# A two-layer recurrent kernel: the selective scan's product with C on GpSimd while expert tiles run

## The chip, the cores and the metric

The program runs on one core of one Trainium2 chip. The metric is the device time of one execution in microseconds. Three runs of the kernel before gave 2524.88 us in the middle, from 2520.57 to 2531.61.

## What is computed

Two layers follow one another on x of shape (4, 1024, 256), all in fp32. Layer 0 is an attention with a Fourier feature map and a gate. Layer 1 is a selective scan (512 channels, 16 states) times the SiLU of a mixture of 8 experts, two experts per token, one after the other. The change lies in layer 1:

```python
def step(h, inp):
    dt_t, B_t, C_t, u_t = inp
    dA = jnp.exp(dt_t[:, :, None] * A)
    h = h * dA + (dt_t * u_t)[:, :, None] * B_t[:, None, :]
    y = jnp.einsum('bcs,bs->bc', h, C_t)
    return (h, y)
...
for i in range(TOP_K):
    eo = _selected_expert(boost, topk_idx[:, :, i], W1, b1, W2, b2)
    outs.append(eo)
    if i < TOP_K - 1:
        boost = boost + ALPHA * eo
...
g = _silu(experts(xn))
x = x + s * g
```

## The kernel before

Time is cut into 8 blocks of 512 tokens (`NBLK`, `TB`), channels into 4 chunks of 128 (`NDI`), two chunks to a half (`UNIT`). One scan step is one (block, half, state): 8 x 2 x 16 = 256 steps.

For a step, `decay` (L588) loads B and C of that state, broadcast over the partitions, into `bcs` (SyncE's queue, 3 buffers) and lets ScalarE make `da` = exp(dt A) (4 buffers). `scan_step` (L606) then gives VectorE four instructions: `h` = dt u times B (L623, 128x1024), two scans (L626, 128x512 each, in place in `h`), and `da` = h times C (L634, 128x1024). `h` has one buffer. Where a block begins a sequence, a small copy keeps the tail of `h` (L631). TensorE adds `da` into `y` by eight accumulating transposes (L637). `y` has one buffer of two PSUM banks; at the end of a unit of 16 steps `end_unit` (L660) multiplies it with the gate on VectorE (L662), and only then the next unit's first matmuls (L617) may write it.

The experts work on slots: `scatter` (L849) writes tokens to rows sorted by expert, with GpSimd's indirect DMA; `all_tiles` (L922) runs 23 slot tiles of 256 rows. For a tile, `fetch` (L870) loads the expert's weights `we` (indirect, GpSimd, 3 buffers) and the rows `xs` (GpSimd's queue, 2 buffers), `hidden_layer` transposes `xs` (`pxs`), copies it (`xst`) and makes `ph` and `ht`; `output_layer` makes `po` on TensorE, adds the bias on VectorE (`es`, L919) and stores it through GpSimd's queue (L920). Then `gather` (L860, buffers `ga`: 8) fetches rows back per token, VectorE makes the second expert's input `x1` (L958, 4 buffers) and updates `xn_all` (L959), `scatter` writes `x1`, and a second round of 23 tiles follows. The last gathers feed L970, a normalization and the output.

`cycle` (L1059) interleaves these: after layer 0 is closed (`l0.close()`), each cycle emits decays up to six steps ahead, two scan steps, up to two pieces of the next unit's preparation (`beside`, L690), and one piece of the experts (`quota=(0, 0, 2, 1)`, L1123), so one slot tile beside two scan steps. That is the order of the program. The framework that builds it orders each engine's queue when the program is built, and among what it takes to be ready it follows the program's order. So `es` of a tile can stand between the two scans of a step, or eight transposes to `y` can be split around `ph`. On the chip each queue runs strictly in that order: an instruction that waits holds all those behind it, DMA issues on SyncE's and GpSimd's queues too.

PSUM's eight banks: `ps_y` 2, `ps_acc` 2 (layer 0's attention alone), `ps_bank` 4.

Of the kernel before, what the change touches and what calls it, by code (L numbers as in the profile page):

```python
# [13 lines left out]
F32 = mybir.dt.float32  # L14
U32 = mybir.dt.uint32
AF = mybir.ActivationFunctionType
ALU = mybir.AluOpType
AX = mybir.AxisListType
PSUM = bass.MemoryType.PSUM
DRAM = bass.MemoryType.DRAM  # L20

P = 128
NB, L, D = 4, 1024, 256
TB = 512
# [10 lines left out]
TS = 256  # L35
# [24 lines left out]
def kernel(  # L60
# [3 lines left out]
    nc = tc.nc  # L64
# [22 lines left out]
    def tokens(ap):  # L87
        return ap.rearrange("(t p) d -> p t d", p=P)
# [7 lines left out]
    def accumulate(ps, pairs):  # L96
        for i, (lhs, rhs) in enumerate(pairs):
            nc.tensor.matmul(ps, lhs, rhs, start=i == 0, stop=i == len(pairs) - 1)  # L98
# [4 lines left out]
    scan = ctx.enter_context(tc.tile_pool(name="scan1", bufs=2))  # L103
    small = ctx.enter_context(tc.tile_pool(name="small", bufs=2))
    ps_y = ctx.enter_context(tc.tile_pool(name="ps_y", bufs=1, space=PSUM))
    ps_acc = ctx.enter_context(tc.tile_pool(name="ps_acc", bufs=2, space=PSUM))
    ps_bank = ctx.enter_context(tc.tile_pool(name="ps_bank", bufs=4, space=PSUM))

    def bank(name):
        return ps_bank.tile([P, TB], F32, name=name, tag="bank")  # L110


    l0 = ExitStack()
    wp = l0.enter_context(tc.tile_pool(name="w0", bufs=1))
    keep = l0.enter_context(tc.tile_pool(name="keep0", bufs=1))
    work = l0.enter_context(tc.tile_pool(name="work0", bufs=7))

    def fetch_x(j):
# [11 lines left out]
        out=bias_s, in_=rows_a.rearrange("a d -> (a d)").partition_broadcast(P)  # L130
# [384 lines left out]
    UNIT = NDI // 2  # L515
# [85 lines left out]
            )  # L601
        decays[j, hf, n] = (bcs, da)

    sums = {}

    def scan_step(j, hf, n):  # L606

        first = j % (L // TB) == 0
        dtu = units[j, hf][1]
        bcs, da = decays.pop((j, hf, n))  # L610
        if n == 0:
            u = blocks[j][1]
            sums[j, hf] = ps_y.tile([P, NT, UNIT * P], F32, name=f"y_{j}{hf}", tag="y")
            for t in range(NT):
                for w in range(UNIT):
                    c = UNIT * hf + w
                    nc.tensor.matmul(  # L617
                        sums[j, hf][:, t, w * P : (w + 1) * P], u[:, c, t * P : (t + 1) * P],
                        skip[:, c, :], start=(t % 2, w) == (0, 0), stop=False,
                    )  # L620
        y = sums[j, hf]
        h = scan.tile([P, UNIT, TB], F32, name=f"h_{j}{hf}_{n}", tag="h", bufs=1)
        nc.vector.tensor_tensor(h, dtu, bcs[:, 0:1, :].to_broadcast([P, UNIT, TB]), ALU.mult)  # L623
        for w in range(UNIT):
            c = UNIT * hf + w
            nc.vector.tensor_tensor_scan(  # L626
                h[:, w, :], da[:, w, :], h[:, w, :],
                0.0 if first else h_tail[:, c, n : n + 1], ALU.mult, ALU.add,
            )
        if first:  # L630
            nc.vector.tensor_copy(  # L631
                h_tail[:, UNIT * hf : UNIT * (hf + 1), n : n + 1], h[:, :, TB - 1 : TB]
            )
        nc.vector.tensor_tensor(da, h, bcs[:, 1:2, :].to_broadcast([P, UNIT, TB]), ALU.mult)  # L634
        for t in range(NT):
            for w in range(UNIT):
                nc.tensor.matmul(  # L637
                    y[:, t, w * P : (w + 1) * P], da[:, w, t * P : (t + 1) * P], ident,
                    is_transpose=True, start=False, stop=(n, t % 2, w) == (NS - 1, 1, UNIT - 1),
                )  # L640
# [49 lines left out]
    def beside(j, hf):  # L690
# [11 lines left out]
        elif j + 1 < NBLK:  # L702
# [8 lines left out]
    slots_in = [dram.tile([NST * TS, D], F32, name=f"slots_in{k}", tag=f"slots_in{k}") for k in range(2)]  # L711
    slots_out = [dram.tile([NST * TS, D], F32, name=f"slots_out{k}", tag=f"slots_out{k}") for k in range(2)]
# [4 lines left out]
            out=slots_in[k].rearrange("(a p) d -> p a d", p=P),  # L717
            in_=blank.unsqueeze(1).to_broadcast([P, NST * TS // P, D]),
# [4 lines left out]
    def needs(later, earlier):  # L723
        tc.add_manual_dep(
            later.ins, earlier.ins.name,
            mybir.DependencyInfo(mybir.DependencyClass.Sync, mybir.DependencyReason.DATA),
        )

    def experts(rp, moe):
# [11 lines left out]
        for e in range(NE):  # L741
# [4 lines left out]
            out=before_m, in_=ones, compare_op=ALU.is_ge, fill=0.0, base=-1,  # L746
# [102 lines left out]
        def scatter(k, t, src):  # L849

            i = nc.gpsimd.indirect_dma_start(
                out=slots_in[k], out_offset=IndirectOffsetOnAxis(ap=slot[:, k, t : t + 1], axis=0),
                in_=src, in_offset=None,
            )
            for o in scattered[k]:
                tc.declare_no_dep(i.ins, o.ins, reason="rows of different tokens")
            needs(i, blanked[k])
            scattered[k].append(i)

        def gather(k, t):  # L860
            g = moe.tile([P, D], F32, name=f"ga_{k}_{t}", tag="ga", bufs=8)
            nc.gpsimd.indirect_dma_start(
                out=g, out_offset=None, in_=slots_out[k],
                in_offset=IndirectOffsetOnAxis(ap=slot[:, k, t : t + 1], axis=0),
            )
            return g
# [3 lines left out]
        def fetch(k, i):  # L870

            w = moe.tile([P, WCAT], F32, name=f"we_{k}_{i}", tag="we", bufs=3)
            nc.gpsimd.indirect_dma_start(
                out=w, out_offset=None, in_=wcat,
                in_offset=IndirectOffsetOnAxis(ap=wrow[:, k, i : i + 1], axis=0),
            )
            xs = moe.tile([P, 2, D], F32, name=f"xs_{k}_{i}", tag="xs")
            got = nc.gpsimd.dma_start(out=xs, in_=tokens(slots_in[k][i * TS : (i + 1) * TS, :]))
            for o in scattered[k]:
                needs(got, o)  # L880
            fetched[k, i] = (w, xs)
# [27 lines left out]
        def output_layer(k, i):  # L909
            w, ht = fetched.pop((k, i))[0], hidden.pop((k, i))  # L910
            we2 = w[:, W1C : W1C + W2C].rearrange("p (f n) -> p f n", n=D)
            b2 = w[:, W1C + W2C + B1C :]
            ps = bank(f"po_{k}_{i}").rearrange("p (u d) -> p u d", u=2)
            for u in range(2):
                accumulate(
                    ps[:, u, :], [(ht[:, f, u * P : (u + 1) * P], we2[:, f, :]) for f in range(NHC)]
                )
            es = moe.tile([P, 2, D], F32, name=f"es_{k}_{i}", tag="es")
            nc.vector.tensor_tensor(es, ps, b2.unsqueeze(1).to_broadcast([P, 2, D]), ALU.add)  # L919
            nc.gpsimd.dma_start(out=tokens(slots_out[k][i * TS : (i + 1) * TS, :]), in_=es)  # L920

        def all_tiles(k):  # L922
            for i in range(2):
                fetch(k, i)
            yield "N"
            for i in range(NST + 1):
                if i:
                    output_layer(k, i - 1)
                if i < NST:
                    hidden_layer(k, i)  # L930
                if i + 2 < NST:
                    fetch(k, i + 2)
                yield "N"

        for t in range(NTT):
            scatter(0, t, xn_all[:, t, :])
            if t % 8 == 7:
                yield "N"
        yield from all_tiles(0)

        def tile_gathers(k):

            got = {}
            for j in range(NBLK + 1):
                if j < NBLK:
                    got[j] = [gather(k, t) for t in range(j * NT, (j + 1) * NT)]
                    yield None
                if j:
                    yield j - 1, got.pop(j - 1)

        for found in tile_gathers(0):
            if found is None:
                yield "N"
                continue
            j, gs = found
            for t, g in zip(range(j * NT, (j + 1) * NT), gs):
                x1 = moe.tile([P, D], F32, name=f"x1_{t}", tag="x1", bufs=4)
                nc.vector.scalar_tensor_tensor(x1, g, 0.5, xn_all[:, t, :], ALU.mult, ALU.add)  # L958
                nc.vector.scalar_tensor_tensor(  # L959
                    xn_all[:, t, :], g, val[:, 0, t : t + 1], xn_all[:, t, :], ALU.mult, ALU.add  # L960
                )
                scatter(1, t, x1)
        yield from all_tiles(1)
        for found in tile_gathers(1):
            if found is None:
                yield "N"
                continue
            j, gs = found
# [150 lines left out]
    rp = ctx.enter_context(tc.tile_pool(name="routes1", bufs=1))  # L1119
    moe = ctx.enter_context(tc.tile_pool(name="moe1", bufs=2))  # L1120
    moe_s.add(experts(rp, moe))
    while not scans.done():
        cycle(quota=(0, 0, 2, 1))  # L1123
    turn_half(NBLK - 1, 1)
# [75 lines left out]
```

## Time and profile before

| what | value |
|---|---|
| median of three runs | 2524.88 us |
| the profiled execution's own time | 2525.45 us |
| its span | 2523.5 us |
| first round of tiles, about | 1600 to 1930 us |
| gathers and second scatters | 1930 to 2060 us |
| second round of tiles | 2060 to 2375 us |
| last gathers, normalization, output | 2375 to 2523.5 us |
| scan steps (L634) in the two rounds of tiles | 49 and 51 |
| loading of `bcs`, issue to landing, in the first round | 5.5 us (median) |
| loading of `we` there | 7.8 us (median) |

The span is what the engines' records cover; the time is what a run reports, 1.95 us more. Starts are counted from the span's start. Busy time of an engine in a stretch against the stretch's length tells how near it is to being the bound there; a chain of waits tells which work ended last at each point.

### The profile page before, as it was taken

To read this page: it belongs to the slowest core of one execution; us is meant where nothing else is said; L and a number is where in the kernel's file an instruction comes from. 1 tells how busy PE (TensorE), PEld (TensorE's weight loads), DVE (VectorE), ACT (ScalarE), POOL (GpSimd) and SP (SyncE) were. 2 spreads that over 40 slices of the span, in tenths; PEclk is the share of its full clock that TensorE was granted. 3 is DMA by queue.
4 is the path that set the end of the run, shared out by engine and by line. 5 is a ranking of instruction groups with operands and counts; after the bars stand their busy time and mean duration, and the time that the engine had idled before them with its cause. 6 is when DMAs were issued, how large, how long until landed. Compare 5 with 4: busy or idle time off the path is not lost.

```text
span 2523.5 us, 25853 instructions
## 1 busy us (share of the span) xinstructions
PE 1894.3 (75%) x9052; PEld 1256.5 (50%) x9052; DVE 2037.3 (81%) x2878; ACT 1334.4 (53%) x2098; POOL 474.0 (19%) x499
## 2 busy tenths in 40 slices
PE   7789795798878888779896865588996458898630
PEld 3335453345554445544455543476784347677520
DVE  4542549999798787887899999699898889989786
ACT  5763457877866767767664343334553333445310
POOL 1001100101000110100001013321224752122241
PEclk8779797699888899979898876799998579999755
DMA  8001123323223223323234463666676447667624
GB/s 287 17 5 46 47 64 84 92 75 78 78 79 106 71 63 82 95 59 96 78 97 131 100 180 99 193 213 219 198 231 196 122 140 224 195 223 227 183 65 158
DMA packets 135777, 315.24 MB, mean 125 GB/s; under 512 B 12240, under 2 KB 39248, under 8 KB 129760
## 3 DMA queue, kind: packets, MB, share of 16 engines
q1 hardware_dynamic: 101456, 168.52, 25.2%
q0 software_dynamic: 34192, 145.08, 16.5%
q8 instruction: 71, 1.16, 0.2%
q14 instruction: 58, 0.48, 0.1%
HBM read 259.56 MB, written 54.00 MB: 124 GB/s over the span
## 4 chain that ended last, share of the span: by engine, by line
DVE 41%; PE 36%; ACT 8%; issue 7%; DMA 5%; POOL 3%; SPq 0%; POOLq 0%; DVEq 0%; ACTq 0%
DVE h L626 14%; DVE h L623 6%; DVE da L634 5%; PE ph L98 4%; PE pa L502 3%; PE ph_b L98 3%; PE po L98 3%; PE y L637 3%; PE py_b L98 2%; PE kv L471 2%; DVE fs_q L442 2%; DVE fs_k L442 2%; DVE u L541 2%; PE pi L98 1%; PE pz L98 1%
## 5 line engine op out<-in xcount | busy, mean ns | idle before, releaser
L637 PE MATMUL y<-ident,da 128*128 128x128 f32 x2048 | 319.0, 303 | 236.0 <-DVE da L634 224.5
L190 ACT ACTIVATE da<-dt,neg_a 128x512 f32<-128x512 f32 x512 | 336.5, 717 | 237.8 <-PE y L637 134.9
L637 PEld LDWEIGHTS y<-ident,da 128*128 128x128 f32 x2048 | 262.2, 156 | 333.3 <-issue 150.6
L626 DVE TENSOR_TENSOR_SCAN h<-da,h_tail,h 128x512 f32<-128x512 f32 x256 | 318.0, 1273 | 32.6 <-ACT da L190 27.8
L626 DVE TENSOR_TENSOR_SCAN h<-da,h 128x512 f32<-128x512 f32 x256 | 302.3, 1213 | 25.5 <-ACT da L190 20.2
L623 DVE TENSOR_TENSOR h<-dtu,bcs 128x1024 f32<-128x1024 f32 x256 | 313.0, 1222 | 5.1
L634 DVE TENSOR_TENSOR da<-h,bcs 128x1024 f32<-128x1024 f32 x256 | 312.5, 1221 | 5.0
L98 PE MATMUL ph<-xst,we 128*128 128x256 f32 x736 | 173.7, 390 | 12.4 <-ACT xst L894 10.9
L98 PE MATMUL po<-we,ht 128*128 128x256 f32 x736 | 172.5, 387 | 3.4 <-DVE es L919 3.1
L182 ACT ACT_TABLE_LOAD x130 | 166.8, 1283 | 2.9 <-PEq L1185 0.8
L98 PEld LDWEIGHTS ph<-xst,we 128*128 128x128 f32 x736 | 138.1, 193 | 39.3 <-ACT xst L894 22.0
L98 PE MATMUL ph_b<-x3t_b,w_b 128*128 128x512 f32 x256 | 134.0, 667 | 25.7 <-DMA w_b<-in_w_dram 15.9
L98 PEld LDWEIGHTS po<-we,ht 128*128 128x128 f32 x736 | 138.7, 195 | 29.2 <-issue 4.3
L906 ACT ACTIVATE ht<-ph,we 128x256 f32<-128x256 f32 x184 | 79.7, 469 | 118.6 <-PE ph L98 117.7
L502 PE MATMUL pa<-fs_q,kvp 128*32 128x512 f32 x512 | 130.3, 736 | 12.9 <-ACT fs_q L190 12.7
L98 PE MATMUL py_b<-w_b,ht_b 128*128 128x256 f32 x512 | 118.9, 392 | 3.7 <-DVE fs_k L442 2.0
L442 DVE SCALAR_TENSOR_TENSOR fs_q<-fs_q,fq 128x512 f32<-128x512 f32 x128 | 81.5, 683 | 46.4 <-ACT fs_q L441 46.0
L442 DVE SCALAR_TENSOR_TENSOR fs_k<-fs_k,fk 128x512 f32<-128x512 f32 x128 | 81.0, 681 | 41.4 <-ACT fs_k L441 41.3
L98 PEld LDWEIGHTS py_b<-w_b,ht_b 128*128 128x128 f32 x512 | 100.1, 197 | 26.9 <-issue 7.2
L441 ACT ACTIVATE fs_q<-fq,round_c 128x512 f32<-128x512 f32 x128 | 79.8, 688 | 62.6 <-PE fq L433 32.2
L471 PE MATMUL kv<-fs_k,v_a 128*32 128x256 f32 x1024 | 88.8, 475 | 27.6 <-ACT fs_k L190 27.6
L433 PE MATMUL fq<-qt_a,bd 32*128 32x512 f32 x256 | 99.5, 717 | 11.8 <-DVE fs_q L442 6.9
(223 smaller groups left out, 3327.6 us busy)
## 6 DMA issues: line engine op xcount, KB each, us to landing
bcs<-bcd SPq DMA_DIRECT2D x256, 512.0 KB, 5.2
x<-in_x_dram POOLq DMA_DIRECT2D x23, 512.0 KB, 6.2
slots_in<-blank SPq DMA_DIRECT2D x2, 5888.0 KB, 31.3
xs<-slots_in POOLq DMA_DIRECT2D x46, 256.0 KB, 4.6
slots_out<-es POOLq DMA_DIRECT2D x46, 256.0 KB, 4.0
w_b<-in_w_dram POOLq DMA_DIRECT2D x16, 512.0 KB, 5.2
w_b<-in_w_dram POOLq DMA_DIRECT2D x32, 256.0 KB, 3.1
x_mid<-x POOLq DMA_DIRECT2D x8, 512.0 KB, 3.4
```

What stands on the lines that cost most here:

```text
L98: nc.tensor.matmul(ps, lhs, rhs, start=i == 0, stop=i == len(pairs) - 1)
L182: nc.scalar.preload_act_table_set({"E": "natural_log_exp_and_others", "S": "silu_and_others"}[which])
L190: in_turn(nc.scalar.activation(out, in_, func, **kw))
L433: nc.tensor.matmul(ps[r], bd_s[rows, par, :], qt[rows, m, :], start=True, stop=True)
L441: nc.scalar.activation(fs[r][:, 0, :], ps[r], AF.Identity, bias=round_c)
L442: nc.vector.scalar_tensor_tensor(fs[r][:, 1, :], fs[r][:, 0, :], -ROUND, ps[r], ALU.add, ALU.subtract)
L471: nc.tensor.matmul(kv[b][r // 2][32 * g : 32 * g + 32, r % 2, :, :], v[:, t, h * DH : (h + 2) * DH], f[:, :, m, par, :], start=(s, t, r % ...
L502: nc.tensor.matmul(pa[b, s][32 * r : 32 * r + 32, :], kvp[b][:, e, 4 * m + r, par, :], fs[r][:, e, :], start=(par, e) == (0, 0), stop=(par ...
L623: nc.vector.tensor_tensor(h, dtu, bcs[:, 0:1, :].to_broadcast([P, UNIT, TB]), ALU.mult)
L626: nc.vector.tensor_tensor_scan(h[:, w, :], da[:, w, :], h[:, w, :], 0.0 if first else h_tail[:, c, n : n + 1], ALU.mult, ALU.add,)
L634: nc.vector.tensor_tensor(da, h, bcs[:, 1:2, :].to_broadcast([P, UNIT, TB]), ALU.mult)
L637: nc.tensor.matmul(y[:, t, w * P : (w + 1) * P], da[:, w, t * P : (t + 1) * P], ident, is_transpose=True, start=False, stop=(n, t % 2, w) ...
```

## The change

Once layer 0 is closed, its two PSUM banks (`ps_acc`, now opened with layer 0's pools) become a buffer `hb`, and a second buffer for `h` is opened for odd states; the room for it comes from `ga` (8 to 6 buffers) and `x1` (4 to 2). From then on dt u B is written to `hb`, and the scans read it there and write `h`. While `all_tiles` runs, from the second of its pieces to the last (`beside_tiles`), the product with C is two GpSimd instructions of 128x512, each after its own scan, in place of one VectorE instruction of 128x1024. Loads of `xs` and stores of `es` go to SyncE's queue.

```diff
-    ps_acc = ctx.enter_context(tc.tile_pool(name="ps_acc", bufs=2, space=PSUM))
...
     l0 = ExitStack()
+    ps_acc = l0.enter_context(tc.tile_pool(name="ps_acc", bufs=2, space=PSUM))
...
-    sums = {}
+    sums, alone, beside_tiles = {}, [], [False]
...
-        h = scan.tile([P, UNIT, TB], F32, name=f"h_{j}{hf}_{n}", tag="h", bufs=1)
-        nc.vector.tensor_tensor(h, dtu, bcs[:, 0:1, :].to_broadcast([P, UNIT, TB]), ALU.mult)
+        if alone and n % 2:
+            h = alone[1].tile([P, UNIT, TB], F32, name=f"h_{j}{hf}_{n}", tag="h")
+        else:
+            h = scan.tile([P, UNIT, TB], F32, name=f"h_{j}{hf}_{n}", tag="h", bufs=1)
+
+        hb = h
+        if alone:
+            hb = alone[0].tile([P, UNIT, TB], F32, name=f"hb_{j}{hf}_{n}", tag="hb")
+        nc.vector.tensor_tensor(hb, dtu, bcs[:, 0:1, :].to_broadcast([P, UNIT, TB]), ALU.mult)
         for w in range(UNIT):
             c = UNIT * hf + w
             nc.vector.tensor_tensor_scan(
-                h[:, w, :], da[:, w, :], h[:, w, :],
+                h[:, w, :], da[:, w, :], hb[:, w, :],
                 0.0 if first else h_tail[:, c, n : n + 1], ALU.mult, ALU.add,
             )
+            if alone and beside_tiles[0]:
+                nc.gpsimd.tensor_tensor(da[:, w, :], h[:, w, :], bcs[:, 1, :], ALU.mult)
...
-        nc.vector.tensor_tensor(da, h, bcs[:, 1:2, :].to_broadcast([P, UNIT, TB]), ALU.mult)
+        if not (alone and beside_tiles[0]):
+            nc.vector.tensor_tensor(da, h, bcs[:, 1:2, :].to_broadcast([P, UNIT, TB]), ALU.mult)
...
-            g = moe.tile([P, D], F32, name=f"ga_{k}_{t}", tag="ga", bufs=8)
+            g = moe.tile([P, D], F32, name=f"ga_{k}_{t}", tag="ga", bufs=6)
...
-            got = nc.gpsimd.dma_start(out=xs, in_=tokens(slots_in[k][i * TS : (i + 1) * TS, :]))
+            got = nc.sync.dma_start(out=xs, in_=tokens(slots_in[k][i * TS : (i + 1) * TS, :]))
...
-            nc.gpsimd.dma_start(out=tokens(slots_out[k][i * TS : (i + 1) * TS, :]), in_=es)
+            nc.sync.dma_start(out=tokens(slots_out[k][i * TS : (i + 1) * TS, :]), in_=es)
...
             yield "N"
+            beside_tiles[0] = True
             for i in range(NST + 1):
...
+            beside_tiles[0] = False
...
-                x1 = moe.tile([P, D], F32, name=f"x1_{t}", tag="x1", bufs=4)
+                x1 = moe.tile([P, D], F32, name=f"x1_{t}", tag="x1", bufs=2)
...
     moe_s.add(experts(rp, moe))
+    alone += [
+        ctx.enter_context(tc.tile_pool(name="hb1", bufs=1, space=PSUM)),
+        ctx.enter_context(tc.tile_pool(name="h1", bufs=1)),
+    ]
```

## The prediction

> **What bounds the kernel now.** I read the page's busy shares first, then busy time by stretch, then both engines' order of time inside the tiles, then waits and transfers. Over the whole span:
>
> ```profile
> PE 1894.3 (75%) x9052; PEld 1256.5 (50%) x9052; DVE 2037.3 (81%) x2878; ACT 1334.4 (53%) x2098; POOL 474.0 (19%) x499
> L623 DVE TENSOR_TENSOR h<-dtu,bcs 128x1024 f32<-128x1024 f32 x256 | 313.0, 1222 | 5.1
> L634 DVE TENSOR_TENSOR da<-h,bcs 128x1024 f32<-128x1024 f32 x256 | 312.5, 1221 | 5.0
> ```
>
> VectorE is the busiest, GpSimd idles 81%, and the product that moves costs 1221 ns a step. But the change acts in the two rounds of tiles alone. Busy time by stretch (length, TensorE, its weight loads, VectorE, ScalarE, GpSimd, granted clock, DMA share, GB/s):
>
> ```profile
> 1600.00:1930.00 330.00, 280.71 (x1448) 234.10 (x1448) 282.50 (x283) 152.68 (x267) 75.71 (x77) 0.93 0.67 209
> 2060.00:2375.00 315.00, 275.58 (x1420) 231.71 (x1420) 289.50 (x289) 150.25 (x263) 63.22 (x66) 0.93 0.66 208
> ```
>
> TensorE (85% and 87%) stands right behind VectorE (86% and 92%): two near-bounds, not one. VectorE in order of time, then TensorE where it is dense:
>
> ```profile
> 1670.71 2.34 DVE L626 TENSOR_TENSOR_SCAN h<-da,h 128x512 f32<-128x512 f32 x2
> 1673.08 0.17 DVE L631 COPY h_tail<-h 128x2 f32<-128x2 f32 x1
> 1673.16 1.22 DVE L634 TENSOR_TENSOR da<-h,bcs 128x1024 f32<-128x1024 f32 x1
> 1674.41 1.22 DVE L623 TENSOR_TENSOR h<-dtu,bcs 128x1024 f32<-128x1024 f32 x1
> 1675.74 2.34 DVE L626 TENSOR_TENSOR_SCAN h<-da,h 128x512 f32<-128x512 f32 x2
> 1678.12 0.17 DVE L631 COPY h_tail<-h 128x2 f32<-128x2 f32 x1
> 1678.19 1.22 DVE L634 TENSOR_TENSOR da<-h,bcs 128x1024 f32<-128x1024 f32 x1
> 1679.45 1.22 DVE L623 TENSOR_TENSOR h<-dtu,bcs 128x1024 f32<-128x1024 f32 x1
> 1680.59 0.68 DVE L919 TENSOR_TENSOR es<-po,we 128x512 f32<-128x512 f32 x1
> 1681.19 2.33 DVE L626 TENSOR_TENSOR_SCAN h<-da,h 128x512 f32<-128x512 f32 x2
> ```
>
> ```profile
> 1864.69 3.62 PE L98 MATMUL po<-we,ht 128*128 128x256 f32 x16
> ...
> 1874.07 3.65 PE L98 MATMUL po<-we,ht 128*128 128x256 f32 x16
> ...
> 1883.53 3.65 PE L98 MATMUL po<-we,ht 128*128 128x256 f32 x16
> ```
>
> A cycle is two steps and a tile. On VectorE it takes 1681.19 - 1670.71 = 10.5 us without a gap. On TensorE, packed, 9.4 us (9.38 and 9.46 between starts of `po`). So where VectorE sets the pace at most 1.1 us a cycle can go before TensorE does. Last, who holds SyncE's queue in the later half (1480 to 2450 us), and the loads of `bcs` in the first round:
>
> ```profile
> SPq L593 <- DVE da L634: 740.6, 121, 19.6
> ```
>
> ```profile
> bcs<-bcd SPq DMA_DIRECT2D x46, 512.0 KB, 5.5
> ```
>
> SyncE spends most of its time with a `bcs` load at its head that waits for the product three steps back; whatever is queued behind it waits too. The whole page puts a long idle time of GpSimd's queue down to `xs` waiting for transposes of the tile before:
>
> ```profile
> POOL xs L878 <- PE pxs L890: 281.1, 36, 21.4
> ```
>
> This wait now goes to SyncE.
>
> **What the Trainium skill says.** "SBUF — State Buffer", Who interferes with whom: a VectorE instruction with two SBUF inputs contends with a GpSimd instruction that reads SBUF, and the later one blocks until the first is done; one with at most one SBUF input doesn't. So the scans, which read `hb` in PSUM, are free of it, and L623 (`dtu` and `bcs`) is not. "PSUM — Partial Sum Buffer", Specifications: VectorE reads and writes PSUM, GpSimd neither; so `h` stays in SBUF. "DMA: Bandwidth & Descriptors", Issuing engines are not separate DMA queues: all queues share the same 16 engines; moving a DMA only saves issue time. The trace of before shows neither contention nor a GpSimd product; the shared engines it shows (67% busy in the tiles, from both queues).
>
> **The change part by part.**
>
> *The product leaves VectorE.* 49 + 51 steps x 1.22 us = 122 us of VectorE's time go in the tiles. What it is worth is set by TensorE. I cut 1640:1920 and 2060:2380 into thirty slices of 20 us; in twelve (1640, 1660, 1680, 1700, 1820, 1880, 2080, 2100, 2120, 2140, 2220, 2320) VectorE is busy 19.3 us or more and TensorE at most 18.5. These 240 us are VectorE's; TensorE is busy 187 us of them. At 9.4 in place of 10.5 us a cycle they become 240 x 9.4 / 10.5 = 215: 25 us gained. Ceiling: TensorE's whole idle time there, 53 us; floor: 0. I take 25. In the other eighteen slices TensorE is the bound or both wait for a chain (the loads of `xt` of 8 us), and I count nothing.
>
> *GpSimd's halves.* No row of before has such an operation (the 128x4 ones of L202 are powers). Price from "GPSIMD Engine Reference", 3.1: 4497 ns for 2048 fp32 elements of an add, so an estimate of 1.12 us for 512; with a fixed part left over, up to 1.35. A cycle has four: 4.5 to 5.4 us, and a `we` issue of 1.5 us (L873), less the two issues of 0.73 us that leave: GpSimd is at most 7 us busy in 9.4. Half 0 runs beside the second scan (1.23 us). Half 1 becomes ready when VectorE goes on to the next L623: they collide on the read port. If L623 goes first, half 1 runs beside the next scan, and VectorE loses 0.1 to 0.3 us a step (3.8 + 0.2 = 4.0 us, plus half of `es`, 4.3, still under TensorE's 4.7). If half 1 goes first each time, L623 waits 1.2 us: 5.05 us as before, and nothing is gained. I take the first, because L623 follows the scan on its own engine without a semaphore.
>
> *dt u B to PSUM, scans from PSUM.* `es`, which reads PSUM, takes 0.68 us for 512 elements against 1.22 us for 1024 in SBUF, so 0.07 us an access, about 0.2 us a step; hidden under TensorE in the tiles, at most 4 us in all outside them (some 22 steps in the gathers and at the end).
>
> *`da`, `y` and `bcs` come later.* The product is ready 1.4 us (free port) to 2.7 us (after L623) after the second scan, against 1.25. Behind it stand TensorE's `y`, ScalarE's next `da` (4 buffers: scans 2.5 + product 2.6 + `y` 1 to 5 + `da` 1.3 to 3 = 7 to 13 us, in four steps of 4.7, covered), and the next load of `bcs` on SyncE. That loop is issue 0.36 + load 5.5 + L623 1.26 + scans 2.46 + product 2.6 + semaphores 0.2 = 12.4 us for 3 buffers: 4.1 us a step (3.7 before), under 4.7 but with only 0.6 left. At a unit's end `y`, L662 and L617 come up to 1.4 us later, six times: 8 us, half of it covered by a tile's matmuls. I take 4 us lost.
>
> *`xs` and `es` to SyncE.* Issue time is nothing (0.36 us each). In SyncE's queue each stands between loads of `bcs`. `xs` of tile i+2 is released by `pxs` of tile i and needed two cycles later: 18.8 - 4.6 = 14 us slack. `es` (two buffers) likewise. They don't suffer; `bcs` behind them can, see the rivals. On GpSimd they no longer stand ahead of `we`, of `branch` and of the halves. At the first round's start `xs` waited there 3.80 us for the last scatter, and a store of `branch` behind it (1601.94) held ScalarE and so VectorE for 13.44 us. Without `xs` it issues about 3 us sooner: 3 us gained.
>
> *Fewer `ga` and `x1`.* From 1929 to 2055 GpSimd issues 64 indirect DMAs almost back to back, about 4 us a token tile, and sets the pace. With two `x1`, the tile after next needs this one's scatter landed: 3.0 us (median) + L958 0.43 + a scan in the way 1.5 = 5 us for two tiles, under the 8 us that GpSimd needs; but VectorE stands at L958 where the scatter is late (8.8 us in three waits already with four). Bounds 0 to 15 us; I take 4 lost.
>
> Sum: -25 - 3 + 4 + 4 = -20 us. Against the profiled execution's 2525.45 (span 2523.5 and 1.95 around it) this gives 2505; the median of the runs, 2524.88, lies 0.6 below, within rounding.
>
> **Rivals.**
>
> A, the full yield: VectorE, relieved, also prepares units sooner and clears L662 for L617 at once, so TensorE's idle time in the twelve slices goes wholly (53 us): about 2477. For it: L617 waited 14.8 us for L662 in 1600:1930. Against: loads of `xt` and the collision of L623 stay.
>
> B, the port takes it back: half 1 wins each time, a step stays 5.05 us, VectorE sets the pace as before. What is left is 3 us gained and 4 + 4 lost: 2530. For it: nothing in the trace excludes it. Against: the order above.
>
> C, the other side: SyncE's queue becomes the bound. The `bcs` loop has 12.4 us of work for three steps. When a wait of `xs` or `es` stands ahead of `bcs`, or 256 KB of either ahead of it on the same ring, the loop grows. From 4.7 us a step, that is an average delay of 1.2 us a cycle, it sets the pace; from 5.25 (2.3 us a cycle) the tiles are slower than before. At 3 us a cycle it is 11.3 us: +0.8 us in some 23 VectorE cycles and +1.9 in some 10 packed TensorE cycles, 37 us; with 4 + 4 - 3 it is 2567, at 2.5 us about 2550. I take 2555. For it: SyncE's head waits above and the mean wait of 7.8 us (281.1 / 36) for `pxs`, inherited. Against: the queues follow the same built order, so most such waits are over before `bcs` is due.
>
> **How the numbers follow.** The likeliest (0.42): 2505, own range 2490 to 2517. A 0.13, B 0.21, C 0.24. A measurement tells 0.5% from no change, 12.6 us. Faster: 0.36 of the likeliest, A, 0.02 of B = 0.51. Same: 0.06, 0.15 of B, 0.01 of C = 0.22. Slower: 0.04 of B, 0.23 of C = 0.27. The range leaves out the best part of A and the worst third of C, some 0.15 in all: 2473 to 2557.
>
> **What would show it.** L634 on VectorE down from 256 to some 156, about 200 GpSimd products of 1.1 to 1.4 us; L623 not longer than 1.3 us (B: up to 2.5). Starts of `po` in packed stretches still 9.4 us apart, and more such stretches; TensorE 90% or more in both rounds. Rounds of tiles some 12 us shorter each; gathers not over 135 us. Wrong if VectorE waits for `bcs` at L623 by more than 1 us a step (C), if L623 lengthens (B), or if L958 waits more than 15 us in the gathers.

## The result, and the profile after

The changed kernel takes 2537.93 us (median of 12 runs, 2529.20 to 2542.60), the kernel before in the same call 2524.52 us. The ratio is 1.0040, 95% interval 1.0026 to 1.0055: by this some 10 us slower (the ratio comes from all runs of both, not from the two medians, which differ by 13.4), where 20 us faster was forecast. The profiled span grew from 2523.5 to 2536.3 us.

Engine shares and groups of instructions of after (x count, busy us, mean ns, idle before):

```profile
PE 1894.2 (75%) x9052; PEld 1254.4 (49%) x9052; DVE 1967.2 (78%) x2782; ACT 1334.4 (53%) x2098; POOL 691.6 (27%) x599
L638 POOL TENSOR_TENSOR da<-h,bcs 128x512 f32<-128x512 f32 x192 | 309.3, 1631 | 183.6 <-DVE h L633 152.5
L630 DVE TENSOR_TENSOR hb<-dtu,bcs 128x1024 f32<-128x1024 f32 x140 | 189.7, 1355 | 34.4 <-DMA bcs<-bcd 33.2
L644 DVE TENSOR_TENSOR da<-h,bcs 128x1024 f32<-128x1024 f32 x160 | 194.9, 1218 | 2.3
L640 DVE COPY h_tail<-h 128x2 f32<-128x2 f32 x128 | 39.1, 305 | 2.8
```

The move happened: 96 of 256 products left VectorE and came back as 192 halves on GpSimd. VectorE's busy time fell by 70 us. Busy time by stretch, the columns as before:

```profile
1600.00:1930.00 330.00, 273.75 (x1395) 227.32 (x1396) 255.94 (x243) 145.54 (x258) 192.51 (x128) 0.92 0.71 214
2060.00:2375.00 315.00, 264.50 (x1349) 221.81 (x1350) 250.07 (x246) 138.60 (x245) 187.68 (x123) 0.91 0.66 202
```

VectorE went from 86% and 92% to 78% and 79%. TensorE did not go up into the room that was made: 83% and 84% here, and where the tiles are under way the same as before (262.6 of the 300 us from 1640, against 263.1 of those from 1630). No engine is a full bound now. The trace gives the time by stage, by the starts of the first and last `es` of each round (us):

| stage | before | after | difference |
|---|---|---|---|
| start to the first `es` of round 1 | 1633.0 | 1645.0 | +12.0 |
| round 1 | 290.4 | 287.8 | -2.6 |
| last `es` of round 1 to first of round 2 (gathers, second scatters, first tile) | 157.7 | 159.5 | +1.8 |
| round 2 | 291.6 | 294.3 | +2.7 |
| last `es` of round 2 to the end | 150.8 | 149.7 | -1.1 |

Each column is one execution. In the kernel before with two `x1` buffers (below), which leaves the program of the rounds as it is, they take 293.6 and 294.0 us, 5.6 us more than in before. A few microseconds in a round therefore mean little by themselves.

So two questions: why the rounds gained nothing from 70 us less of VectorE, and where the 12.7 us outside them come from.

**A step in the rounds.** VectorE of after in order of time, same stretch as before, then GpSimd beside it:

```profile
1672.44 0.67 DVE L929 TENSOR_TENSOR es<-po,we 128x512 f32<-128x512 f32 x1
1673.02 0.99 DVE L640 COPY h_tail<-h 128x2 f32<-128x2 f32 x1
1673.92 1.22 DVE L630 TENSOR_TENSOR hb<-dtu,bcs 128x1024 f32<-128x1024 f32 x1
1675.28 2.33 DVE L633 TENSOR_TENSOR_SCAN h<-da,hb 128x512 f32<-128x512 f32 x2
1677.64 0.23 DVE L640 COPY h_tail<-h 128x2 f32<-128x2 f32 x1
1677.79 1.22 DVE L630 TENSOR_TENSOR hb<-dtu,bcs 128x1024 f32<-128x1024 f32 x1
1679.14 2.33 DVE L633 TENSOR_TENSOR_SCAN h<-da,hb 128x512 f32<-128x512 f32 x2
```

```profile
1671.49 2.50 POOL L638 TENSOR_TENSOR da<-h,bcs 128x512 f32<-128x512 f32 x2 [2.59 <-DVE h L633]
1674.13 1.85 POOL L883 DMA_INDIRECT we<-in_wcat_dram,wrow  x1
1676.58 3.55 POOL L638 TENSOR_TENSOR da<-h,bcs 128x512 f32<-128x512 f32 x2 [0.59 <-DVE h L633]
1680.44 3.55 POOL L638 TENSOR_TENSOR da<-h,bcs 128x512 f32<-128x512 f32 x2 [0.31 <-DVE h L633]
```

A step without `es` now takes 3.86 us (1679.14 - 1675.28), against 5.03 before: for such a step the forecast's 4.0 was close. The pair of halves is 2.50 us where nothing stands against it and 3.55 where L630 started first: the second half then waits for L630's end. Where the second half started first (1673.02), what waits on VectorE is the copy of 128x2: it ends when GpSimd does, 0.99 us in place of 0.17. L630 itself came behind GpSimd in 17 of the 91 steps of the rounds, and then took 1.5 to 3.2 us.

**What TensorE waits for.** The dense step is faster, and the round is not. The waits of TensorE by name in the two rounds (us in total, times, longest; round 1, then round 2), of before and of after:

```profile
PE y L617 <- DVE ys L662: 14.8, 2, 10.3
PE y L637 <- DVE da L634: 12.7, 7, 4.0
...
PE y L617 <- DVE ys L662: 20.6, 3, 10.3
PE y L637 <- DVE da L634: 5.7, 3, 2.3
```

```profile
PE y L617 <- DVE ys L672: 19.8, 3, 6.8
PE y L647 <- POOL da L638: 5.0, 3, 2.1
...
PE y L617 <- DVE ys L672: 22.8, 3, 9.4
PE y L647 <- POOL da L638: 5.0, 3, 2.1
```

Before, TensorE waited 18.4 us for the product and 35.4 us for `ys` at the ends of units; after, 10.0 and 42.6. Sums: 53.8 and 52.6 us. The wait for the product fell by 8.4 us and that at the unit ends grew by 7.2. The kernel with two `x1` buffers, whose rounds have the program of before, differs from before by about as much the other way (25.1 for the product and 28.4 us for `ys`), so these two differences explain nothing alone. All of TensorE's waits come to 67 us before and 69 after.

One unit end of after, all three engines in order of time:

```profile
1689.39 3.56 POOL L638 TENSOR_TENSOR da<-h,bcs 128x512 f32<-128x512 f32 x2 [0.60 <-DVE h L633]
1690.91 0.38 PE L647 MATMUL y<-ident,da 128*128 128x128 f32 x2
1691.95 2.33 DVE L633 TENSOR_TENSOR_SCAN h<-da,hb 128x512 f32<-128x512 f32 x2
1694.20 0.67 DVE L929 TENSOR_TENSOR es<-po,we 128x512 f32<-128x512 f32 x1
1694.79 0.97 DVE L640 COPY h_tail<-h 128x2 f32<-128x2 f32 x1
1695.73 1.23 DVE L630 TENSOR_TENSOR hb<-dtu,bcs 128x1024 f32<-128x1024 f32 x1
1696.87 1.21 DVE L672 TENSOR_TENSOR ys<-ys,y 128x1024 f32<-128x1024 f32 x1
1698.14 1.65 PE L617 MATMUL y<-skip,u 128*128 128x128 f32 x6 [6.84 <-DVE ys L672]
```

The last matmul into `y` ends at 1691.30. `ys` (L672), which frees the only `y` buffer, stands on VectorE behind two scans of the next unit, an `es`, the copy and the next L630: 5.6 us later it starts. The built order puts it there: at the six unit ends of the rounds `ys` stands behind 2, 1, 3, 2, 2 and 3 scan steps of the next unit before, behind 3 each time after, behind 2, 1, 3, 2, 1 and 3 where the product is put back on VectorE (below). In these three kernels the waits go the same way: 35.4, 42.6 and 28.0 us. But the place in the queue alone does not set them: without a product (below) `ys` stands behind 3, 1, 3, 3, 1 and 3 steps and the waits are 11.2 us, because VectorE has those steps behind it sooner. The copy's 0.97 us stands in that queue too. While TensorE stands there, no `y` frees a `da`, and VectorE waits in its turn: its waits at L633 for ScalarE's `da` went from 21.0 to 75.1 us in the two rounds.

**Before the first tiles.** The chain of waits of after at the start of round 1 (start, us, what):

```profile
1600.73 2.40 DMA slots_in<-xn_all,slot
1603.85 13.18 DMA bcs<-bcd
1617.05 1.25 DVE hb L630
```

SyncE's queue, from 1480 to 2450 us:

```profile
SPq L593 <- POOL da L638: 409.8, 90, 10.5
...
SPq L888 <- PE pxs L900: 42.8, 11, 7.3
SPq L888 <- DMA slots_in<-xn_all,slot: 35.4, 1, 35.4
```

The first `xs` waits 35.4 us at the queue's head for the last scatter, with the `bcs` of the next step behind it; that load then lands after 13.18 us, and VectorE has stood still for 31.4 us. Before, it waited 13.44 us there and 9.51 us soon after, both times for ScalarE. From 1480 to 2450 us the wait for `pxs` that SyncE inherited is small: 42.8 us in 11 times, where GpSimd had 281.1 in 36, and in the rounds L630 waits for `bcs` by 1.3 us in all.

**The second scatters.** VectorE at `x1`, over the whole run, in after and in before (`<-DMA slots_in<-x,slot` is the wait for a scatter that still reads one of the buffers):

```profile
L970 DVE SCALAR_TENSOR_TENSOR x<-ga,xn_all 128x256 f32<-128x256 f32 x32 | 13.2, 416 | 20.3 <-DMA slots_in<-x,slot 16.6 <-DMA ga<-slots_out,slot 3.7
```

```profile
L958 DVE SCALAR_TENSOR_TENSOR x<-ga,xn_all 128x256 f32<-128x256 f32 x32 | 13.1, 419 | 15.8 <-DMA slots_in<-x,slot 8.8 <-DMA ga<-slots_out,slot 6.7
```

From the first gather to the last second scatter it is 132.8 us, against 125.5.

### The profile page after: what moved, and what is told of

Same layout as the page of the kernel before. It is cut to its first block, busy times and chain, and to the rows that moved or that the text cites. A ratio compares the mean times of both kernels' runs of the same rounds, so it can differ in the third digit from the quotient of the medians.

```text
span 2536.3 us, 25996 instructions
## 1 busy us (share of the span) xinstructions
PE 1894.2 (75%) x9052; PEld 1254.4 (49%) x9052; DVE 1967.2 (78%) x2782; ACT 1334.4 (53%) x2098; POOL 691.6 (27%) x599
## 4 chain that ended last, share of the span: by engine, by line
DVE 36%; PE 35%; issue 9%; ACT 8%; DMA 7%; POOL 5%; SPq 0%; POOLq 0%; DVEq 0%; ACTq 0%
DVE h L633 11%; PE ph L98 4%; PE pa L502 3%; PE ph_b L98 3%; DVE da L644 3%; PE y L647 3%; PE po L98 3%; DVE hb L630 3%; PE py_b L98 2%; DVE h L630 2%; PE kv L471 2%; POOL slots_in L861 2%; DVE fs_q L442 2%; DVE fs_k L442 2%; DVE u L541 2%
## 5 line engine op out<-in xcount | busy, mean ns | idle before, releaser
L638 POOL TENSOR_TENSOR da<-h,bcs 128x512 f32<-128x512 f32 x192 | 309.3, 1631 | 183.6 <-DVE h L633 152.5
L633 DVE TENSOR_TENSOR_SCAN h<-da,h_tail,hb 128x512 f32<-128x512 f32 x152 | 187.6, 1266 | 56.8 <-ACT da L190 51.8
L630 DVE TENSOR_TENSOR hb<-dtu,bcs 128x1024 f32<-128x1024 f32 x140 | 189.7, 1355 | 34.4 <-DMA bcs<-bcd 33.2
L644 DVE TENSOR_TENSOR da<-h,bcs 128x1024 f32<-128x1024 f32 x160 | 194.9, 1218 | 2.3
L633 DVE TENSOR_TENSOR_SCAN h<-da,hb 128x512 f32<-128x512 f32 x128 | 149.7, 1206 | 27.6 <-ACT da L190 23.3
L98 PEld LDWEIGHTS ph<-xst,we 128*128 128x128 f32 x736 | 138.7, 194 | 35.4 <-ACT xst L904 17.8
L633 DVE TENSOR_TENSOR_SCAN h<-da,h 128x512 f32<-128x512 f32 x128 | 151.0, 1210 | 3.8 <-ACT da L190 2.4
L98 PEld LDWEIGHTS po<-we,ht 128*128 128x128 f32 x736 | 136.9, 192 | 25.1 <-issue 5.1
L630 DVE TENSOR_TENSOR h<-dtu,bcs 128x1024 f32<-128x1024 f32 x116 | 141.6, 1220 | 1.9
L633 DVE TENSOR_TENSOR_SCAN h<-da,h_tail,h 128x512 f32<-128x512 f32 x104 | 129.4, 1271 | 10.5 <-ACT da L190 9.0
L502 PE MATMUL pa<-fs_q,kvp 128*32 128x512 f32 x512 | 128.3, 725 | 12.1 <-ACT fs_q L190 12.0
```

Of the source, the lines that this page charges most:

```text
L502: nc.tensor.matmul(pa[b, s][32 * r : 32 * r + 32, :], kvp[b][:, e, 4 * m + r, par, :], fs[r][:, e, :], start=(par, e) == (0, 0), stop=(par ...
L630: nc.vector.tensor_tensor(hb, dtu, bcs[:, 0:1, :].to_broadcast([P, UNIT, TB]), ALU.mult)
L633: nc.vector.tensor_tensor_scan(h[:, w, :], da[:, w, :], hb[:, w, :], 0.0 if first else h_tail[:, c, n : n + 1], ALU.mult, ALU.add,)
L638: nc.gpsimd.tensor_tensor(da[:, w, :], h[:, w, :], bcs[:, 1, :], ALU.mult)
```

## The experiments

All ratios are against the kernel before, run beside. Theory 1 at the outset: TensorE and what it waits for at the ends of units hold the rounds, so that the product's place is worth nothing, and the loss is the price of room and of the queue (`x1`, `ga`, SyncE). Rivals: the product on GpSimd costs because it collides with L630; or it gains the forecast 25 us, and other parts eat them.

**The product back on VectorE**, the rest of the change kept.

```diff
-            beside_tiles[0] = True
+            beside_tiles[0] = False
```

> The change with the product with C always on VectorE (dt u B to PSUM, two h, fewer ga and x1, SyncE for slot tiles as changed). Theory 1 (the tile rounds are held by TensorE and what it waits for at the ends of units, so the product's place is worth nothing; the loss comes from the other parts): within 8 us of the changed kernel, 2530 to 2546. Theory 2 (the product on GpSimd, 1.8 us a half where it collides with L630, is what costs): back to 2524 or below. Theory of the prediction (the product's leaving gains some 25 us that other parts eat): 2555 to 2565.

Measured: 2537.03 us, 1.0045 (1.0026 to 1.0064): the same as the change, as theory 1 had it. Rounds 288.9 and 290.4 us. TensorE's waits: 21.8 us for the product and 28.0 for `ys`, 49.8 together. The move of the product shows neither gain nor loss (the intervals leave some 6 us either way); the loss lies in the rest of the change. Why the move is worth nothing, this run doesn't say.

**`xs` and `es` back on GpSimd's queue**, and, the other way, **only that move made in the kernel before.**

```diff
-            got = nc.sync.dma_start(out=xs, in_=tokens(slots_in[k][i * TS : (i + 1) * TS, :]))
+            got = nc.gpsimd.dma_start(out=xs, in_=tokens(slots_in[k][i * TS : (i + 1) * TS, :]))
...
-            nc.sync.dma_start(out=tokens(slots_out[k][i * TS : (i + 1) * TS, :]), in_=es)
+            nc.gpsimd.dma_start(out=tokens(slots_out[k][i * TS : (i + 1) * TS, :]), in_=es)
```

> The change with loads of xs and stores of es back on GpSimd's queue. Theory 1 says that the 31 us for which VectorE waits for bcs before the first tiles, behind xs on SyncE, goes, and 5 to 8 us of the time with it: 2529 to 2533. Rival (SyncE's queue is not part of the loss, GpSimd's waits for pxs hold the product instead): 2538 or slower.

> The kernel before with xs and es on SyncE and nothing else. Theory 1: SyncE held by xs at the first scatters costs 4 to 8 us: 2528 to 2533. Rival: no difference, 2522 to 2527.

Measured: 2532.24 us, 1.0028 (1.0017 to 1.0039), and 2524.98 us, 1.0005 (0.9990 to 1.0020). Alone, the move shows no cost, against theory 1. The traces of all kernels of this study suggest why: it has two sides that cancel. With `xs` on SyncE, the first transpose `pxs` to the first `es` of round 1 takes 28.9 to 32.5 us in seven kernels, with `xs` on GpSimd 24.9 to 29.4 in seven: some 4 us lost. From the last second scatter to the first `pxs` of round 2 it is 5.6 to 6.3 us against 7.2 to 11.1, and from the last `es` to the first of the last gathers 7.0 to 8.1 against 10.4 to 11.1: each some 3 us won. The intervals of the change with and without the move overlap, so that the few us between these two aren't settled.

**The buffers alone in the kernel before**: `ga` 6 with `x1` 2, then `x1` 2 only; and `x1` 4 in the changed kernel, with `ga` left at 6.

```diff
-                x1 = moe.tile([P, D], F32, name=f"x1_{t}", tag="x1", bufs=4)
+                x1 = moe.tile([P, D], F32, name=f"x1_{t}", tag="x1", bufs=2)
```

> The kernel before with 6 ga and 2 x1 and nothing else. Theory 1: the gathers and second scatters take 7 us longer (VectorE waits at x1 for scatters): 2528 to 2533. Rival: the 7 us longer gathers of the changed kernel come from elsewhere: 2522 to 2527.

> The kernel before with 2 x1 and nothing else (ga stays at 8). If x1 is what the fewer buffers cost: 2530 to 2537, like both together. If ga is: 2522 to 2527.

> The changed kernel with x1 at 4 buffers again (ga stays at 6). If x1 is what the fewer buffers cost: 2525 to 2531, second scatters about 7 us shorter than in the changed kernel. If ga is: 2535 to 2540.

Measured: 2535.18 us, 1.0039 (1.0024 to 1.0055); 2535.04 us, 1.0032 (1.0019 to 1.0044); and 2531.55 us, 1.0025 (1.0013 to 1.0037). Two `x1` buffers, in an otherwise untouched kernel, lose 8 us (5 to 11), most of the change's 10 (7 to 14). VectorE at `x1` in that kernel, in the stretch of the gathers (1930 to 2070 us):

```profile
L958 DVE SCALAR_TENSOR_TENSOR x<-ga,xn_all 128x256 f32<-128x256 f32 x32 | 13.0, 416 | 22.2 <-DMA slots_in<-x,slot 15.3 <-issue 4.0 <-DMA ga<-slots_out,slot 2.8
```

The wait for scatters goes from 8.8 to 15.3 us, and first gather to last second scatter from 125.5 to 133.4. Over the kernels with two `x1` this is 130.9 to 133.8 us, with four 123.6 to 126.2; only the two kernels with split writes, below, fall outside (130.9 and 135.2 with four). `ga` with six buffers makes the last gathers longer (83.8 to 86.1 us against 79.9 to 80.9 with eight, those two again excepted), but the tail after them is 54.7 to 56.3 us in place of 59, so that about 1 us is left of it. Four `x1` in the changed kernel bring back some 4 of the 10 us, with intervals that overlap; what stays is not named by a run of its own.

**No product beside the tiles**, and **the product's work on GpSimd with nobody waiting for its result.** The first asks what a free product would be worth, the second what GpSimd's work costs by itself. Both leave C out of the sum, and in both the scans write into `da`, so that the buffers of `h` drop out too.

```diff
-        if alone and n % 2:
+        if alone and beside_tiles[0]:
+            h = da
+        elif alone and n % 2:
...
-                nc.gpsimd.tensor_tensor(da[:, w, :], h[:, w, :], bcs[:, 1, :], ALU.mult)
```

> The changed kernel without the product with C while the slot tiles run (no engine makes it: the scans write into da and TensorE adds h instead of h times C), a product that costs nothing. Theory 1 (the rounds of tiles are held by TensorE and the ends of units): rounds still 285 to 294 us from the first es to the last, time 2526 to 2540. Rival (the product itself, wherever it is made, holds the rounds): each round some 12 us or more shorter, 2515 or less.

Added to that for the second:

```diff
+                spare = alone[1].tile([P, TB], F32, name=f"spare_{j}{hf}_{n}{w}", tag="spare")
+                nc.gpsimd.tensor_tensor(spare, h[:, w, :], bcs[:, 1, :], ALU.mult)
```

> no_product with GpSimd's two instructions back beside the tiles, reading the scan's output and C as in the changed kernel, but writing a spare tile that nothing reads; TensorE still adds h without C. GpSimd is as busy and as much in VectorE's way as in the changed kernel, but no matmul waits for it. If contention and GpSimd's time are what takes the gain back (theory 3): 2520 to 2540. If it is that y waits for a product that comes 3.5 us after the scan, and da comes free later (theory 4): 2484 to 2498.

Measured: 2483.59 us, 0.9816 (0.9798 to 0.9834), and 2542.48 us, 1.0056 (1.0034 to 1.0078). Rounds 259.4 and 266.8 us without the product, 290.4 and 294.3 with its shadow. Without it, TensorE's waits in the rounds (round 1, then round 2):

```profile
PE y L617 <- DVE ys L672: 3.4, 2, 2.1
PE po L98 <- DVE h_tail L640: 2.8, 1, 2.8
...
PE y L617 <- DVE ys L672: 7.8, 2, 6.4
```

All its waits fall from 69 to 30 us. Busy time in most of round 1, of after and without the product (columns as before):

```profile
1640.00:1940.00 300.00, 262.63 (x1369) 220.16 (x1367) 243.47 (x229) 140.58 (x248) 179.45 (x119) 0.95 0.72 215
1640.00:1900.00 260.00, 245.72 (x1300) 204.54 (x1299) 213.88 (x227) 134.81 (x238) 24.60 (x24) 0.99 0.77 236
```

So theory 1 falls, and the rival stands that was written beside it: the product itself, wherever it is made, holds the rounds. A free one is worth 56 us there (with whatever the freed buffers of `h` give, which no run separates), and TensorE is then busy 94% of them (494 of 526 us). Of the 56 us, 39 are waits; the rest is TensorE's own busy time, which fell from 512 to 494 us while the granted clock rose from 0.95 and 0.94 in the two rounds to 0.99 and 0.98. Whether the clock is cause or consequence here is not shown; with the shadow, which feeds TensorE the same values, it is back at 0.94 and 0.95. The shadow takes back all of the gain, and more, although no matmul waits for its result: its 192 instructions (mean 1621 ns) hold VectorE and the tiles that they read.

```profile
L641 POOL TENSOR_TENSOR spare<-da,bcs 128x512 f32<-128x512 f32 x192 | 311.1, 1621 | 179.3 <-issue 114.5
```

VectorE's time over the two rounds, against the run without a product: busy 458.4 us in place of 420.0 (91 writes of `hb` 128.3 in place of 111.8, 45 copies to `h_tail` 25.4 in place of 7.5, the rest some 4 us more), idle 126.3 in place of 106.2. Together these are the 58.5 us by which the rounds grow: two thirds longer instructions, one third idle time. This is an account of VectorE's time and does not prove that the collisions set the length of the rounds. The shadow also keeps `da` from ScalarE while GpSimd reads it (ScalarE waits for that 28.2 us in four times over the run), so it can't tell a port from a buffer, and of a late product it excludes only that TensorE waits for it.

**Half of the product**: only half 0 on GpSimd, beside the second scan, which reads PSUM; half 1 on VectorE (and `x1` 4).

```diff
-                nc.gpsimd.tensor_tensor(da[:, w, :], h[:, w, :], bcs[:, 1, :], ALU.mult)
+                eng = nc.vector if w else nc.gpsimd
+                eng.tensor_tensor(da[:, w, :], h[:, w, :], bcs[:, 1, :], ALU.mult)
```

> The changed kernel with x1 at 4 and only the first half of the product on GpSimd, beside the second scan; VectorE makes the second half after it (0.65 us). GpSimd's half no longer meets L630, and the product is there 0.7 us after the last scan. Theory 3 and 4 both: rounds 12 to 20 us shorter than in the changed kernel, 2490 to 2515. Rival (any product on GpSimd takes back what it gives): 2528 to 2535, as with x1 at 4 alone.

Measured: 2527.73 us, 0.9994 (0.9982 to 1.0005): no different from before. Against the changed kernel with four `x1` (1.0025, 1.0013 to 1.0037), which differs in the product alone, it is some 8 us faster: more than the rival allowed, and far from the 2490 to 2515 of both theories. Its trace shows that the collisions have gone (compare 1355 for L630 and 305 for the copy in the rows of after above):

```profile
L630 DVE TENSOR_TENSOR hb<-dtu,bcs 128x1024 f32<-128x1024 f32 x140 | 171.4, 1224 | 32.1 <-DMA bcs<-bcd 32.0
L641 DVE COPY h_tail<-h 128x2 f32<-128x2 f32 x128 | 20.9, 163 | 1.3
```

VectorE does 43 us less product work in the rounds than before, with hardly a collision, and its waits there grow by 45 (36.1 to 80.8). TensorE still waits 42.5 us for `ys`, which stands behind 3, 2, 3, 3, 2 and 3 steps. The collisions are therefore not the only thing that eats the saving. What does, no run names: that it is the unit ends is argued from these waits, and the next run asks what they are worth.

**A second `y` buffer in the kernel before**, in the two banks that the change gives to `hb`: units with `hf == 0` take it once layer 0 is closed. Nothing is moved to GpSimd.

```diff
-            sums[j, hf] = ps_y.tile([P, NT, UNIT * P], F32, name=f"y_{j}{hf}", tag="y")
+            sums[j, hf] = (alone[0] if alone and hf == 0 else ps_y).tile([P, NT, UNIT * P], F32, name=f"y_{j}{hf}", tag="y")
...
+    alone.append(ctx.enter_context(tc.tile_pool(name="y1", bufs=1, space=PSUM)))
```

> The kernel before with a second buffer for y in the two PSUM banks of layer 0's attention, units taking turns. Theory 1: TensorE's waits at L617 for the gate multiply (14.8 and 20.6 us in the two rounds) go; rounds 10 to 20 us shorter each, 2490 to 2510. Rival (TensorE only waits there for work that comes late anyway, VectorE sets the pace): 2520 to 2527.

Measured: 2515.74 us, 0.9946 (0.9930 to 0.9962), faster than both kernels, but less than the forecast 10 to 20 us a round: rounds 290.1 and 283.6 us. L617 no longer waits. TensorE comes to stand one instruction later, at the transposes of `ys` themselves, for less long (round 1, then round 2):

```profile
PE tr_y L223 <- DVE ys L662: 8.9, 2, 7.6
...
PE tr_y L223 <- DVE ys L662: 13.4, 3, 7.7
```

22.3 us in place of 35.4; the waits for the product grow from 18.4 to 27.7, so that all of TensorE's waits come to 62 us in place of 67. The two banks are worth more as a second `y` than as `hb` in any kernel here that makes the product.

**Both together**: the second `y` buffer, and half 0 on GpSimd without a collision, with only the second half of dt u B in a PSUM bank; and its control, the same with half 0 on VectorE.

```diff
+            hb[1] = bank(f"hb_{j}{hf}_{n}")
+            for w in range(UNIT):
+                nc.vector.tensor_tensor(hb[w], dtu[:, w, :], bcs[:, 0, :], ALU.mult)
...
+                eng = nc.vector if w else nc.gpsimd
+                eng.tensor_tensor(da[:, w, :], h[:, w, :], bcs[:, 1, :], ALU.mult)
```

> The kernel before with the second y buffer, and beside the slot tiles half 0 of the product on GpSimd, beside a second scan whose input half lies in PSUM; half 1 stays on VectorE, and dt u B is written in two halves, so that no GpSimd product runs beside an instruction of VectorE with two inputs in SBUF. x1 and ga keep their before counts. VectorE saves 1.22 - 0.74 = 0.48 us a step on the product and pays some 0.2 us for the split write, so 0.28 us x 96 steps = 27 us. If the single y buffer is what kept a contention-free offload from paying (it turned 44 us of saved work into idle time in the run with half of the product), the saving now shows: some 20 to 30 us under the run with the second y buffer alone, ratio 0.983 to 0.988. If the saving is held by something that the y buffer does not touch (ScalarE's da, TensorE, the built order), it stands at the second y buffer's own 0.9946, between 0.991 and 0.998, and VectorE's idle time in the two rounds grows by about what it saves.

> The control: as the run with the second y buffer and half 0 on GpSimd, but both halves of the product on VectorE, so that only the place of half 0 differs. VectorE has 0.2 us more for the split write and 2 x 0.74 - 1.22 = 0.26 us more for the split product, 0.46 us x 96 = 44 us more than with the second y buffer alone. If VectorE's work bounds the rounds once y is doubled, ratio 1.010 to 1.015, and the run with half 0 on GpSimd is 50 to 70 us under it. If something else holds the rounds, part of the 44 us is hidden: 0.997 to 1.005, and the two differ by under 25 us.

Measured: 2586.75 us, 1.0232 (1.0206 to 1.0258), and 2556.53 us, 1.0116 (1.0092 to 1.0140). Both theories of the first run missed it, and its trace says why: it didn't make the experiment that was meant. With dt u B in two instructions, the builder's order puts the half in PSUM first in about every second step, so that the scan of half 0, and GpSimd's product after it, come at the end of the step. TensorE then waits in the rounds 75.8 us for `da` from GpSimd and 18.9 for that from VectorE (59.9 in the control, 27.7 with the second `y` alone), the next write of `h` waits 22.0 us for GpSimd, and the copies to `h_tail` are back at 594 ns. So it stays open whether the saving of the half would show with two `y` buffers; a `hb` of two banks beside two `y` would leave `ps_bank` two, which wasn't tried. What the pair does show: the same half of the product costs 30 us more on GpSimd than on VectorE when it ends the step.

## Why the prediction was wrong

*GpSimd's halves (no loss forecast in the rounds).* The step that failed is "VectorE loses 0.1 to 0.3 us a step (3.8 + 0.2 = 4.0 us, plus half of `es`, 4.3, still under TensorE's 4.7)": because of it the sum holds no term for GpSimd's work. The runs put 58.5 us in its place. By so much the rounds are longer with these halves, nobody waiting for their result, than without them, a little more than the product's leaving gives (56 us).

The price of a half and the order were right: the estimate of 1.12 to 1.35 us met a pair of 2.50, so 1.25 each; L630 mostly goes first and loses 0.20 us a step in the rounds (1425 ns, against 1228 without a product), inside the forecast 0.1 to 0.3. Missing was the copy of 128x2: 0.38 us more in the mean where it occurs (549 against 172 ns, in 45 of the 91 steps), 17 us in the rounds, and some 9 us of small instructions of unit preparation. In all VectorE is busy 464.0 us there, against 420.0 without a product: 0.48 us a step. This alone would still be under TensorE's 4.7 (3.8 + 0.48 + 0.34 = 4.6), so the longer instructions do not account for the whole; how they and the tiles that GpSimd holds come to 58.5 us stays open.

The Trainium skill, "SBUF — State Buffer", Who interferes with whom, exempts VectorE's instructions with at most one SBUF input only outside modes that use two ports, and counts copies and `tensor_scalar` among those that can enter these; the prediction left this condition out. This trace agrees with the page: in the rounds L537, a `tensor_scalar` of 128x512, went from 542 to 1017 ns, and the copy as above.

*The product leaves VectorE (25 us forecast).* Free, it is worth 56 us in the rounds, more than forecast and about the ceiling of 53 for the twelve slices; as forecast TensorE is then the next bound (94% busy). The step was well forecast where nothing else stands in it: 3.86 us against 4.0. (Of the twelve slices that of 1640 has VectorE busy for 19.20 us, not 19.3; nothing hangs on it.) TensorE's waits by name, 18.4 us for the product and 35.4 for `ys` before, would have priced it too low: without the product those for `ys` fell as well.

*Unit ends (4 us forecast, the waits grew by 7.2).* Right in kind, though no larger than the difference between before and the kernel with two `x1`. They are the largest wait of TensorE in the rounds before, 35.4 of 67 us. Rival A had L617 cleared "at once"; in the changed kernel it wasn't (42.6 us), without a product it nearly was (11.2).

*Fewer `ga` and `x1` (4 us forecast, 8 us for `x1` alone).* "5 us for two tiles, under the 8 us that GpSimd needs" was an average; the scatters are uneven, and each late one stops VectorE: 15.3 us of waits in place of 8.8 with two buffers. The bounds of 0 to 15 us held it.

*`xs` and `es` to SyncE (3 us gained at the first round's start forecast).* The gain came at the second round's start and at the last gathers; at the first round's start some 4 us were lost, where the first `xs` took its wait for the scatters into the queue of `bcs`. The prediction named that mechanism in rival C, and priced it only inside the rounds, where `bcs` was hardly late (1.3 us).

*dt u B to PSUM (0.2 us a step forecast, hidden in the tiles).* It cost nothing that shows: L630 takes 1224 ns into PSUM in the run with half of the product, 1220 into SBUF, and a pair of scans 2.33 us from PSUM, 2.34 before.

Of the rivals, B ("the port takes it back", 2530) stands nearest. Its mechanism holds only in part: L630 lost in 17 of 91 steps and not each time, the second half in 59 of 89, the small copy in 13 of 45; a step took 3.86 us and not 5.05, and with the collisions removed most of the saving still turned into idle time. Its number came near partly by luck: fewer `x1` lost 8 us and not 4, and the 3 us won ahead of the first tiles did not come. C did not happen.

The sum after the fact, by stage of the two profiles: rounds +0.1 us in place of -21; gathers and second scatters +7.3, less 5.5 won ahead of and behind them; ahead of the first `es` +12.0, of which 4.5 lie after the first `pxs`, 2.7 between the first scatter and it, and 4.8 before the first scatter (other kernels of this study stand there anywhere from 1548.4 to 1564.5 us, so these 4.8 belong to no part of the change alone).

## What to carry to other kernels

Price both ends of a move apart. One kernel leaves the moved work out, and shows what the relieved engine's time is worth (56 us here, where its waits by name said 18.4); the other gives the work to the new engine with nobody waiting for it, and shows what that takes back (58.5 us). Where two engines hand a single buffer back and forth, look at what stands in the queue ahead of the instruction that frees it, and try spare memory there: as a second `y` the two banks gained some 14 us. Before elementwise work moves from VectorE to GpSimd, list every VectorE instruction that will run beside it, tiny copies too, and let GpSimd's run only beside those that read PSUM (worth some 8 us here); and count what is taken away to make the room (8 us for two `x1` buffers).

## What the runs showed of the hardware

A product of 128x512 on GpSimd, both inputs in SBUF, takes 1.25 us beside scans with one input in PSUM, and some 2.3 us when VectorE starts an instruction with two SBUF inputs just before it. The Trainium skill, "Perfetto Trace Analysis", Optimizing Scalar/DVE Operations, says that moving work between these two engines may not help because of the shared port; here 192 such halves that nobody waited for cost the rounds 58.5 us, against 56 us that their absence gave.

A copy of 128x2 on VectorE, 0.17 us by itself, took 0.99 us where it started beside such a product (1673.02) and ended with it. In all 13 cases of the rounds in which the copy took over 0.3 us it ended with GpSimd's product; in four of them it waited for both halves and took 1.96 to 2.04 us. What it pays is the time that GpSimd still needs, whatever its own size.
